# Second group's context and normalized x: turned by 128-byte loads and VectorE's 32x32 transposes in place of TensorE

## Chip, core and metric

The kernel runs on one core of a Trainium2 chip. The metric is the device time of one execution in microseconds (us), as the median of several runs. Everything is float32. The engines of the core are TensorE (PE in the profile; PEld is its weight load), VectorE (DVE), ScalarE (ACT), GpSimd (POOL) and SyncE (SP, which issues all DMA transfers of this kernel on one queue).

## What is computed

A cross-attention block: 8 sequences of 256 tokens (`x`), with a context of 256 tokens each, width 512, 16 heads of 32, and a hidden layer of 2048. Cut to what matters:

```python
B, LQ, _ = hidden_states.shape
residual = hidden_states
x = layer_norm(hidden_states, ln1_w, ln1_b)
q = (x @ q_w + q_b).reshape(B, LQ, H, HD).transpose(0, 2, 1, 3)
k = (encoder_hidden_states @ k_w + k_b).reshape(B, LK, H, HD).transpose(0, 2, 1, 3)
v = (encoder_hidden_states @ v_w + v_b).reshape(B, LK, H, HD).transpose(0, 2, 1, 3)
scores = jnp.einsum('bhqd,bhkd->bhqk', q, k) * scale
scores = jnp.where(mask, scores, mask_value)
attn = jax.nn.softmax(scores, axis=-1)
out = jnp.einsum('bhqk,bhkd->bhqd', attn, v)
out = out.transpose(0, 2, 1, 3).reshape(B, LQ, D)
hidden = out @ cproj_w + cproj_b + residual
y = layer_norm(hidden, ln2_w, ln2_b)
y = jax.nn.gelu(y @ fc_w + fc_b, approximate=True)
return hidden + y @ proj_w + proj_b
```

## The kernel before

The eight sequences are worked in two groups of four (g = 0 and 1), 1024 tokens each. For each group: the context and the normalized x are brought into a layout with the features on the partitions ("turned"), then come the projections k, v and q, sixteen attention units, the output projection `o`, the second layer norm, and the two layers `fc` and `pd`. The matrix products are done with Strassen's scheme of seven products (`quad`): a product is called `k1_0_P1` (group 1, part 0, product 1) and so on, and the sums it needs are called `c1t1`, `x1t2`, `kws1`, `fw0s1`, `z0t1` (outer sums) and `fw0i1_1`, `y0i1_1`, `z0i1_1` (inner sums). Product results are evicted from PSUM by DVE or ACT (`_t1`, `_c11`, `_c22` and so on), and some later additions may go to DVE or POOL.

An attention unit has a number of three digits (group, head group, sequence): `s101` are its scores on PE, `ev` the evictions with the mask on ACT, `mx`, `mt`, `mc` and `fold` the maximum over the keys on DVE and ACT, `md` a store of that maximum to memory and `mm` a load that spreads it over all partitions, `less` the subtraction on POOL or DVE, `exp` the exponential on ACT, `av` the value product and the row sums on PE, `r` and `att` the division on DVE. Three further units are scored before a unit's `av`.

How the turn was done for group 1: the context came as eight tiles of 128 tokens (`ct1_0` to `ct1_7`, rows of 2 KB). `turned` (L711) runs for each of four 128-wide blocks of features (a) and each half of the tokens (L) four 128x128 transposes on PE against the identity into one PSUM bank (L728, operation `turn_c1_aL`), and an eviction of 128x512 to SBUF (L608, `c1_aL`, ACT or DVE). For x, tiles `xt1_0` to `xt1_7` are normalized in token layout (`norm_x1`, L807 on ACT or L809 on DVE) and then turned in the same way (`turn_x1_aL`), with the layer norm's weight and bias applied in the eviction (`x1_aL`, L764 on ACT, L766 on DVE).

A second way to turn is already there, `moved` (L732), used for y of group 1: the normalized tiles are stored to memory (`yd1_0` to `yd1_7`), read back in pieces of 32 features (128 bytes) so that each 32x32 block lies on the right partitions (`yb1_ca`, sixteen loads of 128 KB), turned block by block on DVE (`yT1_cL`, L747), and scaled in place (`y1_cL`, L751 on ACT, L753 on DVE). All loads are issued at L595, all stores at L601.

What sets the order: the string `PROGRAM` lists all operations in one sequence, with a letter for the engine where there is a choice (V for DVE, A for ACT, G for POOL). Each engine, and SP, takes its operations in this order; an operation that waits holds back all behind it on its engine. `PLACES` gives each buffer its slot in SBUF or its PSUM bank. Both tables are written out in the file.

Of the kernel before, what the change touches and what calls it, by code (L numbers as in the profile page):

```python
# [124 lines left out]
cq0_00_0 cq0_00_1 kw00 vw00 cq0_01_0 rows8 cq0_01_1 mk turn_c0_00 cq0_10_1 turn_c0_10 c0_00:V cq0_10_0 c0_10:A  # L125
cq0_11_0 small k0_0_P1 vw01 rows4 v0_0_P1 vw11 rows6 cq0_11_1 turn_c0_11 xt0_0 turn_c0_01 c0_11:V v0_1_P1 rows1
rows3 turn_c0_30 rows2 k0_1_P1 c0_30:V vw10 c0_01:V rows7 rows0 v0_0_t1:V turn_c0_20 rows5 turn_c0_21 c0_20:V kw01
turn_c0_31 c0t1:V fw0_11_1 v0_0_P2 c0_31:A kw10 c0_21:A vws1:V v0_1_t1:A kw11 fw0_10_0 stats_x0_00 c0t2:G v0_1_P2
v0_0_c11 xt0_7 mk~1 fw0_00_0 k0_0_P2 fw0_00_1 v0_1_c11 fw0_11_0 vws2:V kws3:V fw0_10_1 v0_1_P6 vws4:V xt0_3 kws1:V
fw0_01_1 xt0_1 cols v0_0_P6 v0_1_t2:A cols~1 fw0_01_0 c0t3:V xt0_2 fw1_00_0 c0t4:V k0_1_P2 v0_0_t2:A vd0_0_11  # L130
k0_1_t1:A xt0_5 fw0i1_1:V k0_0_t1:A kws2:V fw1_11_0 k0_0_P7 stats_x0_31 fw1_00_1 fw0s3:V k0_1_P6 fw0s1:V fw0i2_1:V
k0_1_P7 fw0i5_3:G k0_1_t2:A fw0s2:V k0_1_P5 fw0i7_1:V fcd0_6_False stats_x0_01 fw0i6_3:G xt0_6 fw0i5_1:V
fcd0_7_False k0_1_c11 fw0i6_1:G k0_0_P6 fw1_11_1 k0_0_c11 fw0i5_2:G fw1_01_0 stats_x0_21 fw0i6_2:G kd0_0_11
aggr_x0_01 aggr_x0_00 v0_1_P5 fw0i1_2:V k0_0_t2:A fw0s4:G k0_1_t3:A k0_1_c22 k0_0_P5 stats_x0_30 aggr_x0_30
stats_x0_10 fw0i6_4:G stats_x0_11 k0_1_P4 fw0i7_2:G k0_0_t3:A fcd0_6_True xt0_4 kws4:V fw1_01_1 aggr_x0_10
aggr_x0_11 v0_1_t3:V v0_0_P5 xt1_2 fw0i1_4:V aggr_x0_31 fcd0_5_False eps_x0_1 k0_0_c22 pow_x0_1 aggr_x0_21 k0_0_P4
fw0i2_3:V fw0i2_2:V eps_x0_3 nb_x0_1 eps_x0_0 stats_x0_20 fw0i2_4:G norm_x0_10:A fw0i7_3:V v0_0_t3:A v0_1_P3
fcd0_2_True pow_x0_0 k0_0_c21 norm_x0_11:A fw1_10_1 pow_x0_3 qw11 nb_x0_0 aggr_x0_20 nb_x0_3 eps_x0_2 k0_1_P3 qw10
fw0i7_4:V norm_x0_30:A pow_x0_2 qw00 norm_x0_00:A fw1i1_1:V qw01 fw1i4_3:G norm_x0_01:A fw1_10_0 k0_0_P3 nb_x0_2
fw0i5_4:G k0_1_c12:A norm_x0_20:A fw1i1_3:G fcd0_5_True turn_x0_00 fcd0_7_True fw0i1_3:G norm_x0_21:A k0_0_c12:V  # L140
turn_x0_30 kd0_1_11 qws1:G x0_00:A v0_0_P3 fcd0_1_True norm_x0_31:A kd0_1_12 vws3:V ct1_7 k0_1_c21 fw1i4_1:G
turn_x0_20 kd0_0_21 turn_x0_10 x0_30:V kd0_1_21 turn_x0_01 x0_10:A x0_20:V ct1_1 turn_x0_31 x0_01:A turn_x0_21
qws2:V turn_x0_11 v0_1_c12:V q0_0_P1 x0_11:A fw1i2_1:V fw1i4_2:V x0_31:A fw1i4_4:V v0_0_c12:V x0_21:A q0_1_P1
x0t1:V x0t2:V q0_1_P2 q0_1_t1:A x0t3:V q0_0_P2 fw1s1:V fw1i2_2:V q0_0_t1:A fcd1_5_False q0_1_P6 fw1i5_3:G xt1_3
fw1i2_3:V fcd1_4_True qws3:G q0_1_c11 ku031 q0_0_c11 q0_0_P6 x0t4:V s000 q0_0_t2:A fw1s3:V q0_0_P7 fw1s2:V ev000_31
fcd1_7_False q0_1_t2:A ev000_11 fw1i5_1:V fcd1_6_False fw1i6_1:G q0_0_P5 fcd0_3_False fw1i5_2:V fw1s4:G q0_1_P5
# [202 lines left out]
tr1_23 pd13_P4 out1_31:V pd17_11~1:G so1_33 pd12_P4 pd17_12~1:G so1_31 pd13_c21 tr1_13 so1_00 tr1_22 so1_03 pd14_t1  # L349
so1_01 pd14_P6 pd12_c21 tr1_10 tr1_12 out1_10:V pd14_P2 out1_11:V out1_21:V so1_10 pd14_t2 so1_13 pd14_P5 so1_32  # L350
so1_02 so1_21 pd14_P7 so1_12 pd14_t3 pd14_c11 so1_23 so1_30 so1_20 pd14_P3 pd14_c22 so1_11 so1_22 pd14_P4 pd14_c12
turn_o00 pd14_c21 ot00 turn_o10 turn_o11 ot10 turn_o01 ot11 st0 ot01 st1
"""

PLACES = """
# [1114 lines left out]
```

## Time and profile before

| | |
|---|---|
| median of three runs | 677.62 us (677.07 to 677.84) |
| profiled execution, its own time | 679.25 us |
| its span, first to last instruction | 677.5 us |
| granted TensorE clock | 0.999 |
| PE, DVE, ACT, POOL busy | 666.5, 589.9, 334.8, 347.6 us |
| DMA packets, bytes | 173033, 140.64 MB |
| packets under 512 bytes | 83713 |

In the profile a row of a group of instructions names line, engine, operation, what is written from what, the shapes and the count; then the busy time and the mean of one in ns; then the idle time of the engine just ahead of them and what ended it. Names of tiles are those of buffers, and a slot of SBUF goes by the name of its first user, so that `kw` or `xt` can stand for a later tile in the same place. In the row of a window, each engine has its busy time and in brackets its instructions; behind them stand the granted clock, the mean busy share of the sixteen DMA engines and the GB/s that they moved.

### The profile page before, as it was taken

The numbers are of one execution on the slowest core, as the hardware profiler recorded it, in microseconds if no ns is written. First come the engines' busy times: TensorE is split into PE (matmuls) and PEld (weight loads), VectorE is DVE, ScalarE is ACT, GpSimd is POOL, SyncE is SP. The second block draws the span as 40 slices with busy tenths as digits, with TensorE's granted clock in tenths as the row PEclk, the third lists the DMA queues.
The fourth block names the chain that finished last, engine by engine and source line by source line (L and its number), as shares of the span: only waits on it lengthen the run. The fifth ranks groups of instructions, "written<-read, shape, count | busy, mean of one in ns | idle before, by whom it ended". The sixth has DMA issues, their size and how long they took to land.

```text
span 677.5 us, 11498 instructions
## 1 busy us (share of the span) xinstructions
PE 666.5 (98%) x4001; PEld 498.2 (74%) x4001; DVE 589.9 (87%) x981; ACT 334.8 (49%) x691; POOL 347.6 (51%) x329
## 2 busy tenths in 40 slices
PE   9999999999999999999999999999999999999997
PEld 7656474478544776767687788888888888888885
DVE  1979989789999999999999999988677869999794
ACT  1244588678899979965874582011021003930000
POOL 0282563632879997689686924221398332300150
PEclk9999999999999999999999999999999999999999
DMA  7898885522445457796878769698998778434966
GB/s 239 290 303 315 292 319 191 184 87 79 134 165 164 141 159 236 244 288 218 257 226 270 225 164 284 173 290 306 138 240 262 183 175 224 118 90 124 228 164 117
DMA packets 173033, 140.64 MB, mean 208 GB/s; under 512 B 83713, under 2 KB 133425, under 8 KB 172977
## 3 DMA queue, kind: packets, MB, share of 16 engines
q1 hardware_dynamic: 172976, 139.92, 70.6%
q8 instruction: 32, 0.52, 0.3%
q14 instruction: 25, 0.20, 0.1%
HBM read 102.00 MB, written 37.88 MB: 206 GB/s over the span
## 4 chain that ended last, share of the span: by engine, by line
PE 73%; DVE 13%; ACT 5%; issue 3%; DMA 3%; POOL 2%; SPq 0%; DVEq 0%; POOLq 0%; ACTq 0%
PE pd_X L641 14%; PE fc_X L641 12%; PE pd_W L641 7%; PE fc_W L641 6%; DVE mx L1004 4%; PE av L641 4%; PE k_X L641 4%; PE pd_Y L641 4%; PE fc_Y L641 4%; PE v_X L641 3%; ACT pr L621 2%; PE s L641 2%; PE o_X L641 2%; PE k_W L641 2%; DVE h L632 2%
## 5 line engine op out<-in xcount | busy, mean ns | idle before, releaser
L621 ACT ACTIVATE pr<-s,cols 128x256 f32<-128x256 f32 x256 | 103.9, 482 | 28.2 <-PE s L641 19.6
L1029 POOL TENSOR_TENSOR pr<-pr,mm 128x512 f32<-128x512 f32 x80 | 100.5, 1284 | 8.3 <-DMA mm<-md 8.2
L1209 ACT ACTIVATE h<-h,cols 128x256 f32<-128x256 f32 x128 | 53.8, 497 | 51.1 <-DVE h L632 51.0
L1004 DVE TRANSPOSE_TENSOR_REDUCE mx<-pr 128x32 f32<-128x1024 f32 x64 | 77.5, 1223 | 1.6 <-DMA md<-mx 0.8
L1032 ACT ACTIVATE pr<-pr 128x1024 f32<-128x1024 f32 x64 | 66.5, 1061 | 8.7 <-POOL pr L1029 5.3
L632 DVE TENSOR_TENSOR h<-fc_X,h 128x512 f32<-128x512 f32 x80 | 53.0, 681 | 10.2 <-PE fc_X L641 8.9
L641 PE MATMUL av<-pr,ones 128*32 128x256 f32 x512 | 34.2, 384 | 2.3 <-ACT pr L1032 1.9
L632 DVE TENSOR_TENSOR h<-fc_W,h 128x512 f32<-128x512 f32 x48 | 32.0, 678 | 2.9 <-PE fc_W L641 2.9
L630 POOL TENSOR_TENSOR z1i<-z1t,z1t 128x512 f32<-128x512 f32 x2 | 2.5, 1268 | 55.8 <-DVE z1t L632 55.8
L1024 DVE TENSOR_TENSOR pr<-pr,mm 128x1024 f32<-128x1024 f32 x24 | 29.6, 1253 | 0.5 <-DMA mm<-md 0.5
L641 PEld LDWEIGHTS av<-pr,ones 128*32 128x32 f32 x512 | 14.1, 109 | 20.4 <-issue 6.0
L807 ACT ACTIVATE xn_y<-hid,rs_y 128x512 f32<-128x512 f32 x12 | 9.4, 812 | 37.6 <-DVE rs_y L799 32.4
L1011 ACT COPY mx<-mx 32x64 f32<-32x64 f32 x96 | 23.3, 243 | 7.9 <-DVE mx L1008 5.6
L641 PE MATMUL pd_W<-z1i,pl 128*128 128x256 f32 x104 | 24.4, 379 | 0.0
L641 PE MATMUL pd_X<-z0i,pl 128*128 128x256 f32 x96 | 22.5, 380 | 0.0
L641 PE MATMUL pd_X<-z1i,pl 128*128 128x256 f32 x96 | 22.2, 381 | 0.0
L641 PEld LDWEIGHTS pd_W<-z1i,pl 128*128 128x128 f32 x104 | 19.8, 190 | 2.7
L1012 DVE TENSOR_REDUCE mx<-mx 32x32 f32<-32x256 f32 x32 | 18.4, 574 | 3.8 <-ACT mx L1011 3.8
L641 PE MATMUL pd_W<-z0i,pl 128*128 128x256 f32 x88 | 20.7, 380 | 0.2 <-issue 0.2
L641 PEld LDWEIGHTS pd_X<-z1i,pl 128*128 128x128 f32 x96 | 18.0, 190 | 3.1 <-issue 0.4
L641 PEld LDWEIGHTS pd_X<-z0i,pl 128*128 128x128 f32 x96 | 18.2, 190 | 2.9 <-DVE po L853 0.4
L632 POOL TENSOR_TENSOR po<-po,e 128x256 f32<-128x256 f32 x12 | 10.3, 874 | 18.4 <-DVE e L632 11.6
(585 smaller groups left out, 1815.6 us busy)
## 6 DMA issues: line engine op xcount, KB each, us to landing
mm<-md SPq DMA_DIRECT2D x32, 512.0 KB, 4.5
pl<-prd SPq DMA_DIRECT2D x63, 256.0 KB, 3.4
fl<-fcd SPq DMA_DIRECT2D x33, 256.0 KB, 4.8
fw<-in_L_xattn_fc_w_dram SPq DMA_DIRECT2D x16, 256.0 KB, 5.0
pw<-in_L_xattn_proj_w_dram SPq DMA_DIRECT2D x32, 128.0 KB, 3.6
hid<-in_x_dram SPq DMA_DIRECT2D x8, 512.0 KB
hd<-hid SPq DMA_DIRECT2D x8, 512.0 KB, 5.5
fcd<-fw0i SPq DMA_DIRECT2D x7, 512.0 KB, 7.2
```

The lines of the kernel that those rows point to most:

```text
L621: lambda e: nc.scalar.activation(to(), of_(), AF.Identity, bias=bias(), scale=1.0))
L630: nc.gpsimd.tensor_tensor(to()[:, ts(k, 512)], in0()[:, ts(k, 512)], in1()[:, ts(k, 512)], op)
L632: E[e].tensor_tensor(to(), in0(), in1(), op)
L641: nc.tensor.matmul(o(), l(), r(), start=first, stop=True, skip_group_check=True)
L807: nc.scalar.activation(tile_of(xn), f(), AF.Identity, bias=tile_of(rs)[:, 4 + i : 5 + i], scale=tile_of(rs)[:, 2 + i : 3 + i])
L1004: T.op(f"mx{u}_{h}", [("DVE", 1.126)], [(pr[h], None)], [(mx, [h])], lambda e, h=h: nc.vector.tensor_reduce(tile_of(mx)[:, 0:64].rearrange ...
L1011: lambda e, a=a: nc.scalar.copy(tile_of(mx)[0:32, 64 + 64 * a : 128 + 64 * a], tile_of(mx)[32 * a : 32 * a + 32, 64:128]))
L1012: T.op(f"fold{u}", [("DVE", 0.38)], [(mx, [2, 3, 4, 5])], [(mx, [6])], lambda e: nc.vector.tensor_reduce(tile_of(mx)[0:32, 320:352], tile_ ...
L1024: nc.vector.tensor_tensor(p_, p_, m_[:, :, None, :].to_broadcast([P, 2, 2, S]), ALU.subtract)
L1029: E[e].tensor_tensor(p_, p_, at(M, j)[:, None, :].to_broadcast([P, 2, S]), ALU.subtract)
L1032: lambda e, h=h: nc.scalar.activation(tile_of(pr[h]), tile_of(pr[h]), AF.Exp), table="exp")
L1209: lambda e, f=f, b=b, c=c: nc.scalar.activation(at(h[f][b], c), at(h[f][b], c), AF.Gelu_apprx_tanh, bias=col(c_fcb + f * 4 + c), scale=1.0 ...
```

## The change

`attention_inputs` no longer calls `turned` for group 1.

- The context of group 1 is read by a new function, `fetched`: sixteen loads of 128 KB straight from the input, in pieces of 128 bytes (`cb1_ca`; c is the block of 128 features, a the 32 features within it), and eight DVE transposes of 128x512 in 32x32 blocks (`cT1_cL`), which write the turned tensor. The eight tile loads, eight groups of PE transposes and eight evictions are gone.
- The normalized x of group 1 goes through `moved`: eight stores (`xd1_0` to `xd1_7`, 256 KB each), sixteen loads of 128-byte pieces (`xb1_ca`), each of which needs all eight stores, eight DVE transposes (`xT1_cL`), and eight scalings in place (`x1_cL`, six on ACT and two on DVE).
- `PROGRAM` and `PLACES` are other tables: 2951 operations in place of 2927, in another order from the third on, 222 of the kept ones on another engine (from POOL to DVE 88, DVE to POOL 84, DVE to ACT 31, ACT to DVE 19).

```diff
+    def fetched(g, tag, src):
+        R = [[Buf(f"{tag}{g}_{J}{L}", "Q", 4) for L in range(2)] for J in range(2)]
+        for c in range(4):
+            q = Buf(f"{tag}b{g}_{c}", "Q", 4)
+            for a in range(4):
+                load(f"{tag}b{g}_{c}{a}", q, [a], lambda q=q, a=a: tile_of(q)[32 * a : 32 * a + 32].rearrange("p (t j) -> p t j", j=32),
+                     lambda a=a, c=c: src[ts(g, 1024), :].rearrange("(t i) (b a j) -> b a i t j", i=32, b=4, a=4)[c, a], 0.33, lead=2.0)
+            for L in range(2):
+                r, j = R[c // 2][L], c % 2
+                T.op(f"{tag}T{g}_{c}{L}", [("DVE", 0.6)], [(q, None)], [(r, [2 * j, 2 * j + 1])],
+                     lambda e, q=q, r=r, j=j, L=L: nc.vector.transpose(at(r, j, 1, 512), at(q, L, 1, 512)))
+        return R
...
-        ct = token_quarters(g, "c", ef) if g == 0 else token_tiles(g, "c", ef)
         if g == 0:
+            ct = token_quarters(g, "c", ef)
             biases()
-        C = turned(g, "c", ct if g == 0 else [(b, lambda b=b: tile_of(b)) for b in ct], plain)
+        C = turned(g, "c", ct, plain) if g == 0 else fetched(g, "c", ef)
...
-        X = turned(g, "x", xn, scaled(c_ln1w, c_ln1b))
+        X = moved(g, "x", xn, c_ln1w, c_ln1b) if g else turned(g, "x", xn, scaled(c_ln1w, c_ln1b))
...
 PROGRAM = """
-cq0_00_0 cq0_00_1 kw00 vw00 cq0_01_0 rows8 cq0_01_1 mk turn_c0_00 cq0_10_1 turn_c0_10 c0_00:V cq0_10_0 c0_10:A
+cq0_00_0 cq0_00_1 mk cq0_10_1 cq0_10_0 rows8 rows2 vw00 turn_c0_10 cq0_01_0 turn_c0_00 c0_10:A cq0_01_1 c0_00:V rows6
```

Three places show the order. The first is PE, between the scores of unit 022 and those of unit 010, before. `ps_c_11` and `ps_c_01` are the PSUM banks of the turned context, `v_1_W` a product of v of group 0.

```order
L641 MATMUL s_3_889<-q_0_22_733,k_0_22_491 128x256
L728 MATMUL ps_c_11_900<-ident,xt_5_409 128x128
L728 MATMUL ps_c_11_900<-ident,xn_x_10_527 128x128
L728 MATMUL ps_c_11_900<-ident,ct_6_814 128x128
L728 MATMUL ps_c_11_900<-ident,k_0_22_491 128x128
L641 MATMUL v_1_W<-vw_259,c0t_399 128x256 x4
L728 MATMUL ps_c_01_922<-ident,xt_5_409 128x128
```

The same place now:

```order
L640 MATMUL s_3_888<-q_0_22_738,kw_320 128x256
L640 MATMUL v_1_W<-vws_323,c0t_339 128x256 x4
L640 MATMUL v_0_W<-vw_294,c0t_360 128x256 x4
L640 MATMUL v_1_W<-vw_294,c0t_360 128x256 x4
L640 MATMUL s_0_949<-q_0_11_680,xt_2_370 128x256
```

All eight groups of transposes of the context stood here; now three products stand between the two scores.

The second is SP, around the maximum of unit 001 (`md_154`, stored, and the `mm` read back from it), before. `pw` is a weight of the second layer, `ku` keys that are read back.

```order
L595 DMA ku_1508<-kd_1_22_129 128x256
L595 DMA ku_1510<-kd_1_11_126 128x256
L595 DMA ku_1523<-kd_0_22_125 128x256
L601 DMA md_154<-mx_1446 32x32
L595 DMA mm_1603<-md_154 128x1024
L595 DMA pw_00_1605<-in_L_xattn_proj_w_dram 128x2x128
```

And now, with the stores of x (`xd_162`) and the loads of its pieces (`xb_c`):

```order
L600 DMA xd_162<-xt_7_1098 128x512
L600 DMA xd_162<-kw_282 128x512
L594 DMA ku_1473<-kd_1_11_126 128x256
L594 DMA vu_1477<-vd_0_12_131 128x2x128
L600 DMA md_154<-mx_1429 32x32
L594 DMA xb_2_1505<-xd_162 32x32x32
L594 DMA xb_0_1513<-xd_162 32x32x32
L594 DMA ku_1515<-kd_1_21_128 128x256
L594 DMA xb_2_1505<-xd_162 32x32x32
L594 DMA mm_1521<-md_154 128x1024
```

The read-back of the maximum now stands behind three loads of pieces, the first of which needs the last store of x.

The third is DVE, where the last of x was evicted before (`x_11` and `x_01` from their PSUM banks):

```order
L632 TENSOR_TENSOR v_1_11_1503<-v_1_Y,v_1_11_1503 128x512
L1024 TENSOR_TENSOR pr_0_1413<-pr_0_1413,mm_1603 128x1024
L766 TENSOR_SCALAR x_11_1655<-ps_x_31_1640,cols 128x512
L766 TENSOR_SCALAR x_01_1663<-ps_x_01_1650,cols 128x512
L1024 TENSOR_TENSOR pr_1_1399<-pr_1_1399,mm_1603 128x1024
```

and where it is turned now, ahead of the first product of q of group 1:

```order
L759 STREAM_TRANSPOSE x_01_1693<-xb_1_1676 128x512
L759 STREAM_TRANSPOSE x_00_1781<-xb_1_1676 128x512
L765 TENSOR_SCALAR x_00_1781<-x_00_1781,cols 128x512
L631 TENSOR_TENSOR xt_1_1149<-v_0_W,xt_1_1149 128x512
L759 STREAM_TRANSPOSE x_11_1740<-xb_3_1743 128x512
L1024 TENSOR_REDUCE mx_1714<-mx_1714 32x32
L759 STREAM_TRANSPOSE x_10_1664<-xb_3_1743 128x512
```

Two evictions stood here; now four transposes and a scaling do, each transpose behind the loads of its block.

More of the change, by code (lines that the diff above doesn't have):

```diff
@@ L130 @@
[L130 to L134, printed above, removed]
@@ L350 @@
[L350 to L352 removed]
+cq0_00_0 cq0_00_1 mk cq0_10_1 cq0_10_0 rows8 rows2 vw00 turn_c0_10 cq0_01_0 turn_c0_00 c0_10:A cq0_01_1 c0_00:V
+rows6 cq0_11_1 cq0_11_0 turn_c0_20 vw01 turn_c0_30 c0_20:V small v0_1_P1 kw10 mk~1 c0_30:V rows5 vw10 v0_0_P1 kw00
```

668 lines of the change are left out of this document (337 added, 331 removed).

## The prediction

> **What bounds the kernel now.** I read the page first: the span, the busy shares, the slices.
>
> ```profile
> span 677.5 us, 11498 instructions
> PE 666.5 (98%) x4001; PEld 498.2 (74%) x4001; DVE 589.9 (87%) x981; ACT 334.8 (49%) x691; POOL 347.6 (51%) x329
> DVE  1979989789999999999999999988677869999794
> DMA  7898885522445457796878769698998778434966
> ```
>
> TensorE (PE) is busy 98% of the span, VectorE (DVE) 87%, and in the middle of the run DVE stands at nine tenths too. The busy shares of five stretches (length, then PE, PEld, DVE, ACT, POOL, granted clock, DMA share, GB/s) show which is where.
>
> ```profile
> 0.00:160.00 160.00, 158.42 (x919) 97.67 (x920) 129.85 (x232) 92.25 (x187) 68.07 (x76) 1.00 0.71 239
> 256.00:340.00 84.00, 82.06 (x744) 57.68 (x743) 81.62 (x152) 65.65 (x130) 67.18 (x71) 1.00 0.79 249
> 440.00:660.00 220.00, 219.97 (x1011) 190.60 (x1010) 184.25 (x300) 43.57 (x92) 76.44 (x74) 1.00 0.77 195
> 85.00:105.00 20.00, 19.57 (x152) 13.48 (x151) 17.91 (x28) 17.21 (x44) 14.95 (x15) 1.00 0.85 309
> 140.00:160.00 20.00, 19.86 (x143) 15.60 (x142) 17.93 (x39) 15.34 (x34) 2.07 (x3) 1.00 0.24 80
> ```
>
> Up to 160 us PE is full and DVE has 30 us free; from 256 to 340 us DVE has 2.4 us free and PE 1.9; from 440 us PE is full and DVE has 36 us free. So PE sets the pace at both ends, and DVE holds it in the late scores of group 1. The waits of PE are small; the longest two end on the softmax and on a POOL addition (total, times, longest):
>
> ```profile
> PE av L641 <- ACT pr L1032: 1.9, 2, 1.4
> PE fc_W L641 <- POOL h L632: 0.8, 1, 0.8
> ```
>
> **What PE loses.** The timeline of PE (start, duration) around the last transposes of x, and the chain of waits (last row) later:
>
> ```profile
> 160.47 0.27 PE L728 MATMUL ps_x<-ident,xt 128*128 128x128 f32 x1
> 162.10 0.27 PE L728 MATMUL ps_x<-ident,kws 128*128 128x128 f32 x1
> 162.21 3.62 PE L641 MATMUL v_X<-vws,c 128*128 128x256 f32 x16
> 165.76 1.15 PE L641 MATMUL s<-q,ku 32*128 32x256 f32 x16
> 166.84 1.99 PE L641 MATMUL v_W<-vw,c1t 128*128 128x256 f32 x8
> 168.67 1.89 PE L641 MATMUL v_W<-xt,c1t 128*128 128x256 f32 x8
> 451.50 10.36 PE pd_X L641 x48
> ```
>
> Sixteen transposes run from 160.47 to 162.21, 0.109 us each. The change removes 64 (two tensors, eight groups of four): 7.0 us. Against this, the new order goes more often between full products and the row-wise scores or column-wise value products: I count 107 such changes in it, 97 before. A step of eight takes 1.73 us inside a run (10.36 for 48) and 1.83 us behind a score (166.84 to 168.67), so a change costs 0.1 us and ten more cost 1.0. PE has 6.0 us less to do.
>
> **What DVE and ACT get.** The groups of instructions (busy, mean ns of one):
>
> ```profile
> L747 DVE STREAM_TRANSPOSE y<-yb 128x512 f32<-128x512 f32 x8 | 5.4, 688 | 0.0
> L608 DVE COPY c<-ps_c 128x512 f32<-128x512 f32 x8 | 5.4, 680 | 13.6 <-PE ps_c L728 13.6
> L766 DVE TENSOR_SCALAR x<-ps_x,cols 128x512 f32<-128x512 f32 x5 | 3.9, 797 | 0.4 <-PE ps_x L728 0.4
> L608 ACT COPY c<-ps_c 128x512 f32<-128x512 f32 x8 | 4.6, 588 | 15.8 <-PE ps_c L728 15.8
> L751 ACT ACTIVATE y<-y,cols 128x512 f32<-128x512 f32 x7 | 5.5, 811 | 20.5 <-DVE y L747 20.5
> L753 DVE TENSOR_SCALAR y<-y,cols x1: 499/499/499, 494.8 to 494.8; 128x512 f32<-128x512 f32 x1
> ```
>
> The same turn exists already for y of group 1, so its price is in the trace. DVE gains 16 transposes at 0.69 (11.0) and two scalings at 0.50 (1.0), and loses three evictions of c at 0.68 and three of x at 0.80 (4.4): 7.6 us more. ACT loses five copies at 0.59 and keeps the scalings, six instead of five at 0.81: it has half its time free. The rest of the order pays DVE's 7.6 back: `less` 24 to 22 on DVE, `xb` 5 to 2, the outer sums `z` 30 to 25, more of others. Adding all DVE instructions of each order with the durations of their groups gives 635.8 us before and 634.7 now (durations overlap, so the sum stands above the 589.9 busy). In total DVE is even; what matters is where.
>
> ```profile
> 256.73 1.15 PE L641 MATMUL s<-vws,k 32*128 32x256 f32 x16
> 336.32 1.15 PE L641 MATMUL s<-q,k 32*128 32x256 f32 x16
> ```
>
> These are the scores of unit 101 and of unit 133, the last, 79.6 us apart: the stretch that DVE holds. In it DVE has 83.4 us of durations before and 87.2 now (four more statistics of y and three aggregates, two more first evictions of fc), so 0.954 us of time for each, and 83.2 us now: 3.6 longer, where PE has 2.8 more. Ahead of unit 101 PE has 16 groups of transposes fewer (-7.0), one step of 1.73 fewer and eight changes of mode more (+0.8): -7.9. DVE has 4.2 us fewer durations there, so it does not take that back. Behind unit 133 PE has one step of 0.87 fewer: -0.9. Sum: -7.9 + 3.6 - 0.9 = -5.2.
>
> **What the DMA queue and SP get.** Issue to landing, and three windows of 5 us around y's turn:
>
> ```profile
> yb<-yd SPq DMA_DIRECT2D x16, 128.0 KB, 4.4
> yd<-xn_y SPq DMA_DIRECT2D x7, 256.0 KB, 5.4
> 470.00:475.00 5.00, 5.00 (x25) 4.41 (x24) 2.39 (x3) 0.47 (x1) 2.19 (x2) 1.00 0.93 301
> 480.00:485.00 5.00, 5.00 (x25) 4.41 (x24) 3.30 (x7) 0.00 (x0) 0.47 (x1) 1.00 1.42 146
> ```
>
> With whole rows a full queue moves 301 GB/s, with the 128-byte pieces 146. A tensor of 2.1 MB so takes 14.4 us instead of 7.0. Context of group 1 costs the queue 7.4 us more; x a store of 7.0 and a load of 14.4, 21.4 more. The x pieces fall where the queue is busy 24% (140 to 160 us, above), so they lie beside other work; without that room they would cost the 21.4. The context pieces fall ahead of 105 us, into a queue at 85%: 15% of some 100 us is free, twice what they need. Ahead of `xb1_22` SP now waits for the last `xd1` to land, 5.4 us after its issue; two PE steps (3.5 us) lie between, so SP stands about 2 us, and behind it the pieces, `ku031` and the maximum of unit 001 (`mm001`). Fourteen PE steps and scores, some 21 us, lie between `mm001` and its `av001`: hidden, or 2 us if not.
>
> The tight place is the first softmax:
>
> ```profile
> 82.43 7.01 DMA md<-mx
> 89.52 0.32 SPq L595 DMA_DIRECT2D mm<-md  x1
> 93.55 4.97 POOL L1029 TENSOR_TENSOR pr<-pr,mm 128x512 f32<-128x512 f32 x4 [1.34 <-DMA mm<-md]
> 102.65 1.86 PE av L641 x32
> L1032 ACT ACTIVATE pr<-pr 128x1024 f32<-128x1024 f32 x64 | 66.5, 1061 | 8.7 <-POOL pr L1029 5.3 <-DVE pr L1024 3.3
> ```
>
> Store and load of the maximum of unit 000 pass a queue full of stores: 7.0 us, then 4.0. POOL subtracts 5.0, ACT's exponential takes 1.1: ready at 99.6, wanted at 102.65, 3.0 us spare. Eight of the removed groups of transposes stood in that gap: the work that is taken away was itself the cover. Before, PE had three scores, eight turns and four steps between `mm000` and `av000` (3.3 + 3.5 + 6.9 = 13.7 us); now it has two scores and five steps (2.2 + 8.6 = 10.8). 2.9 of the 3.0 are gone. If the queue is as late as before, PE loses nothing; if it is 1 to 3 us later, PE stands that long; if it is earlier (fewer stores lie ahead of this maximum than before), still nothing is won. I take 0.6, ends 0 and 3.
>
> The forecast: -5.2 + 0.6 = -4.6 us. The profiled run took 679.25 us for its span of 677.5; the sum is made against the span, 672.9, which is 674.6 as a profiled run and 677.62 - 4.6 = **673.0** against the median.
>
> **Rivals.**
> *PE alone counts.* DVE follows in the late scores, since it got 30 us of room early and can work ahead. Then -6.0 and no new stall: 677.6 - 6.0 = 671.6; 670 if the 1.9 us of old waits at value products go too. For it: equal DVE totals. Against: 2.4 us free in 84.
> *DVE takes it back.* If DVE needs not 0.954 but full durations in the stretch (+3.8) and again behind it, where up to the first steps of `pd02` DVE's durations run 7.3 us ahead of PE's, 0.7 before, then another 6.6 x 0.93 = 6.1 us come on top: 678, no change. For it: additions with both inputs in SBUF are dearer here when POOL works:
>
> ```profile
> L632 DVE TENSOR_TENSOR h<-h,e 128x512 f32<-128x512 f32 x5 | 4.7, 930 | 0.0
> ```
>
> 0.93 against 0.68 for evictions; five outer sums go from POOL to DVE. [...] Against: DVE has 36 us free behind 440.
> *The queue falls behind (slower).* Place: `md` and `mm` of units 000 to 022, behind 128-byte pieces and stores of `fcd`. It decides once `mm000` lands more than 0.1 us later than before; then everything behind `av000` inherits it, since PE takes its work in order. If all 7.4 us of extra queue time ahead of 105 us arrive at `av000`, PE loses 7.3 there; and x's last loads have two value products, a step and a score (6.3 us) between them and the first product of q, for 4.4 of landing and two transposes on DVE: another 1 to 2 if they are as late. 677.6 - 6.0 + 7.3 + 1.5 = 680.4, with an open end upward. For it: 7.0 us landing of 4 KB at 82 us; queue above 0.85. Against: 15% free.
> [...]
>
> *The change doesn't do what it says.* Excluded: the 64 transposes are gone from PE's list.
>
> **How the numbers follow.** Forecast 0.45 (671.5 to 675.5), PE alone 0.12 (669.5 to 671.5), DVE takes it 0.17 (675.5 to 679), queue 0.26 (679 to 688). A measurement here tells 0.2%, 1.4 us, from no change: faster is below 676.3. That is forecast, PE alone and a sixth of DVE's: 0.60; same is most of DVE's and a little of the queue's, 0.13; slower 0.27. The range 669.5 to 684 leaves out a twentieth below and a tenth above; the likeliest's own is 671.5 to 675.5.
>
> **What would show it.** PE busy near 660 and 3937 matmuls; scores of unit 101 near 249 us and of unit 133 near 332; DVE over 97% busy between them; a wait of PE at the first `av` under 1 us; 128-byte loads landing in 4 to 5 us, x's in a queue under 80%. Wrong would be: PE idle over 4 us ahead of 110 us (queue), or unit 133 later than 335 us (DVE), or unit 101 later than 252.

## The result, and the profile after

The changed kernel takes 670.76 us (median of nine runs, 668.47 to 675.55) where the kernel before takes 677.23 (nine runs, 676.17 to 678.58): a ratio of 0.9913, 95% interval 0.9888 to 0.9938, so 4.2 to 7.6 us faster: 6.5 us between the medians, 5.9 by the ratio, which is one of means. The forecast was 673.0. The profiled execution took 672.14 us for a span of 670.3, against 679.25 and 677.5 before.

The page of the changed kernel, the same lines as before:

```profile
span 670.3 us, 11469 instructions
PE 658.5 (98%) x3937; PEld 491.4 (73%) x3937; DVE 590.8 (88%) x986; ACT 340.0 (51%) x700; POOL 358.8 (54%) x323
DVE  2989799989999999999999999998688868897985
DMA  8998988578647447787788876978977986538756
```

PE does 64 matmuls fewer and is busy 8.0 us less, DVE is busy 0.9 us more: the turn has moved from an engine that is full to one that was "even" in total. The span is 7.2 us shorter. Where, is read from three windows, cut at the scores of unit 101 and of unit 133 (length, then busy time of PE, PEld, DVE, ACT and POOL, clock, DMA share, GB/s). Before:

```profile
0.00:256.73 256.73, 253.47 (x1673) 157.54 (x1673) 222.92 (x376) 177.64 (x374) 148.83 (x135) 1.00 0.62 205
256.73:336.32 79.59, 77.65 (x714) 54.26 (x713) 77.21 (x147) 62.03 (x122) 62.89 (x67) 1.00 0.78 245
336.32:677.50 341.18, 335.34 (x1617) 286.37 (x1616) 289.79 (x460) 95.12 (x198) 135.85 (x128) 1.00 0.76 201
```

The changed kernel:

```profile
0.00:248.78 248.78, 245.25 (x1602) 147.92 (x1602) 221.31 (x371) 178.43 (x376) 148.33 (x132) 1.00 0.76 225
248.78:333.31 84.53, 80.93 (x725) 57.15 (x724) 80.31 (x153) 64.20 (x124) 69.03 (x73) 1.00 0.77 242
333.31:670.30 336.99, 332.36 (x1613) 286.32 (x1612) 289.14 (x464) 97.39 (x202) 141.43 (x121) 1.00 0.77 203
```

Up to unit 101 it gains 7.95 us, in the late scores it gives 4.94 back, and behind unit 133 it gains 4.19 again. In the first stretch PE's records fall by 71 and its busy time by 8.2: the gain there is PE's work. In the middle both PE (+3.3) and DVE (+3.1) have more to do. PE's 11 records more there are those that the two other stretches lose beside the 64 transposes (7 and 4): work that the new order has moved, not new work. Behind unit 133 PE has four records fewer, 0.9 us, but 4.2 us less time: that is the part that needs explaining.

The first value product, where the forecast feared the queue. The timeline of the changed kernel (start, duration; the store of the maximum of unit 000, its load, the subtraction, the second exponential, the product):

```profile
78.67 0.70 SPq L600 DMA_DIRECT2D md<-mx  x1
82.23 0.34 SPq L594 DMA_DIRECT2D mm<-md  x1
86.12 5.02 POOL L1041 TENSOR_TENSOR pr<-pr,mm 128x512 f32<-128x512 f32 x4 [0.94 <-DMA mm<-md]
92.31 1.06 ACT L1044 ACTIVATE pr<-pr 128x1024 f32<-128x1024 f32 x1
94.36 1.07 PE L640 MATMUL av<-pr,ones 128*32 128x256 f32 x16
```

The same exponential before:

```profile
100.88 1.10 ACT L1032 ACTIVATE pr<-pr 128x1024 f32<-128x1024 f32 x1
```

Before, it ended at 101.98 and the product began at 102.65: 0.7 us to spare, not the 3.0 that the prediction worked out from POOL's end. Now it ends at 93.37 and the product begins at 94.36 without a wait: 1.0 us to spare. The load is issued 3.6 us after the store instead of 7.1. So the cover did shrink (from the store to the product 15.7 us instead of 20.2), but the maximum's way through the queue shrank with it.

The 128-byte loads (KB each, median us from issue to landing), the transposes and DVE's two scalings of x (busy, mean ns, idle before), in the changed kernel:

```profile
cb<-in_ctx_dram SPq DMA_DIRECT2D x16, 128.0 KB, 4.0
xb<-xd SPq DMA_DIRECT2D x16, 128.0 KB, 3.6
```

```profile
L742 DVE STREAM_TRANSPOSE c<-cb 128x512 f32<-128x512 f32 x8 | 5.2, 674 | 0.0
L759 DVE STREAM_TRANSPOSE x<-xb 128x512 f32<-128x512 f32 x8 | 5.4, 686 | 0.0
L765 DVE TENSOR_SCALAR x<-x,cols 128x512 f32<-128x512 f32 x2 | 2.1, 1026 | 0.0
```

The transposes cost what was forecast (0.69 us), the loads land a little sooner than the 4.4 us of y's; a scaling on DVE took 1.03 us, twice its price.

### The profile page after: what moved, and what is told of

The parts are those of the page before. It is cut to its first block, busy times and chain, and to the rows that moved or that the text cites. A ratio compares the mean times of both kernels' runs of the same rounds, so it can differ in the third digit from the quotient of the medians.

```text
span 670.3 us, 11469 instructions
## 1 busy us (share of the span) xinstructions
PE 658.5 (98%) x3937; PEld 491.4 (73%) x3937; DVE 590.8 (88%) x986; ACT 340.0 (51%) x700; POOL 358.8 (54%) x323
## 4 chain that ended last, share of the span: by engine, by line
PE 73%; DVE 15%; DMA 3%; ACT 3%; issue 2%; SPq 1%; POOL 0%; DVEq 0%; ACTq 0%
PE pd_X L640 14%; PE fc_X L640 13%; PE pd_W L640 7%; PE fc_W L640 7%; DVE mx L1016 4%; PE v_X L640 4%; PE pd_Y L640 4%; PE av L640 3%; PE fc_Y L640 3%; PE k_X L640 2%; PE s L640 2%; PE q_X L640 2%; PE o_X L640 2%; PE k_W L640 2%; PE o_W L640 2%
## 5 line engine op out<-in xcount | busy, mean ns | idle before, releaser
L1041 POOL TENSOR_TENSOR pr<-pr,mm 128x512 f32<-128x512 f32 x84 | 110.0, 1342 | 27.7 <-DMA mm<-md 20.4
L631 POOL TENSOR_TENSOR tq<-tq,rq 128x512 f32<-128x512 f32 x9 | 11.8, 1313 | 32.9 <-PE pd_X L640 13.0
L640 PE MATMUL fc_X<-y1i,fl 128*128 128x256 f32 x96 | 24.4, 382 | 0.1
L607 ACT COPY e<-fc_X 128x512 f32<-128x512 f32 x5 | 2.9, 581 | 40.9 <-DMA fl<-fcd 31.6
L763 ACT ACTIVATE y<-y,cols 128x512 f32<-128x512 f32 x6 | 4.9, 812 | 35.9 <-DMA yb<-yd 20.0
L629 POOL TENSOR_TENSOR z0t<-h,z0t 128x512 f32<-128x512 f32 x6 | 7.6, 1282 | 27.6 <-DVE z0t L631 19.1
L640 PE MATMUL fc_W<-y1i,fl 128*128 128x256 f32 x84 | 20.8, 380 | 0.0
L640 PEld LDWEIGHTS fc_X<-y1i,fl 128*128 128x128 f32 x96 | 17.9, 190 | 3.4 <-DVE fl L607 0.5
L1396 POOL TENSOR_TENSOR hid<-hid,cb 128x1024 f32<-128x1024 f32 x6 | 15.4, 2578 | 6.6 <-DMA hid<-in_x_dram 6.6
L640 PE MATMUL pd_X<-z0i,pl 128*128 128x256 f32 x80 | 18.6, 379 | 0.0
```

What stands on the lines that cost most here:

```text
L629: nc.gpsimd.tensor_tensor(to()[:, ts(k, 512)], in0()[:, ts(k, 512)], in1()[:, ts(k, 512)], op)
L631: E[e].tensor_tensor(to(), in0(), in1(), op)
L640: nc.tensor.matmul(o(), l(), r(), start=first, stop=True, skip_group_check=True)
L1041: E[e].tensor_tensor(p_, p_, at(M, j)[:, None, :].to_broadcast([P, 2, S]), ALU.subtract)
L1396: lambda e, v=v: E[e].tensor_tensor(v(), v(), cb.t[:, None, :].to_broadcast([P, 2, D]), ALU.add), lock=True)
```

## The experiments

Twelve kernels, all but one built from the changed kernel; each was timed against the kernel before on the same chip. The chips differ from group to group, so a distance from the changed kernel is taken from the ratios (their difference, in us of 677.2), which fixes it to about 2 us: the last column.

| run | edit, in short | median us | ratio to before, 95% interval | later than the change, us |
|---|---|---|---|---|
| (the change) | | 670.76 | 0.9913 (0.9888 to 0.9938) | 0 |
| e1 | PE work added | 682.19 | 1.0069 (1.0055 to 1.0084) | +10.6 |
| e2 | new DVE transposes twice | 685.54 | 1.0126 (1.0106 to 1.0145) | +14.4 |
| e3 | whole rows for 128-byte pieces | 672.03 | 0.9921 (0.9903 to 0.9938) | +0.5 |
| e4 | pieces twice | 682.64 | 1.0080 (1.0058 to 1.0101) | +11.3 |
| e5 | late DVE work added | 684.18 | 1.0100 (1.0087 to 1.0114) | +12.7 |
| e6 | late DVE work taken away | 672.41 | 0.9918 (0.9898 to 0.9938) | +0.3 |
| e7 | two stores ahead of the first maximum | 671.17 | 0.9901 (0.9886 to 0.9917) | -0.8 |
| e8 | context half undone | 676.17 | 0.9984 (0.9974 to 0.9994) | +4.8 |
| e9 | 16 additions divided as before | 675.15 | 0.9961 (0.9944 to 0.9977) | +3.3 |
| e10 | the kernel before, additions divided as after | 676.45 | 0.9983 (0.9971 to 0.9995) | |
| e11 | one late store moved | 675.75 | 0.9965 (0.9952 to 0.9978) | +3.5 |
| e12 | all 16 additions on GpSimd | 673.01 | 0.9925 (0.9902 to 0.9949) | +0.8 |

### e1: is TensorE's time what counts?

```diff
-                for j in range(2)
+                for j in ((0, 0, 0, 0, 0, 1) if p == 1 and name[:2] in ("k1", "q1") else (0, 1))
```

> The changed kernel with 16 more matmuls of TensorE: the first 128x512 product of the first step of each k and q of group 1 is done five times instead of once (same result), 16 x 0.43 = 6.9 us, near the places where the transposes stood. If TensorE sets the pace up to unit 101 and its lost time counts in full: the score of unit 101 at 248.8 + 6.9 = 255.7, and the end later by 5 to 7 us, near 676 to 678. If VectorE holds the run from 105 us on, it uses the time to get ahead and most comes back in the late scores: the end later by 0 to 3 us, 671 to 674.

```profile
0.00:262.22 262.22, 259.12 (x1633) 154.18 (x1634) 220.46 (x371) 178.47 (x376) 150.56 (x131) 1.00 0.72 213
262.22:345.62 83.40, 80.59 (x726) 56.46 (x725) 79.54 (x153) 64.13 (x124) 69.16 (x73) 1.00 0.77 246
```

The same windows, up to unit 133. The price in the expectation was half of the true one: one 128x512 product is two records of 0.43 us, so 16 of them are 32 records (3969 in all against 3937) and 13.9 us of busy time in the first stretch. The score of unit 101 is 13.4 us later and the end 12.2 in the profiled pair, 10.6 by the ratios: between three quarters and nine tenths of the added work arrive at the end. The late scores take 83.4 us, 0.1 less than in any other run that leaves them as they are (83.5 to 84.8), although DVE had 13 us longer for what lies ahead of them. TensorE's time counts for the most part; VectorE does not use the time to get ahead by more than that.

### e2, e3, e4: do DVE's transposes and the small pieces lie beside other work?

e2, in `fetched`, and in `moved` for x:

```diff
-                     lambda e, q=q, r=r, j=j, L=L: nc.vector.transpose(at(r, j, 1, 512), at(q, L, 1, 512)))
+                     lambda e, q=q, r=r, j=j, L=L: [nc.vector.transpose(at(r, j, 1, 512), at(q, L, 1, 512)) for _ in range(1 if tag == "y" else 2)])
```

> The changed kernel with each of the 16 new VectorE transposes done twice: 16 x 0.69 = 11.0 us of VectorE more, half of it at 89 to 103 us (21 us free in the first 105), half at 158 to 177 us, where VectorE is 91 to 98% busy. If TensorE sets the pace: the context half is hidden, of the x half one or two us show, the end at 671 to 673. If VectorE holds the pace from 105 us on: 5.5 x 0.95 = 5.2 us more at least, 676; with both halves 10.5 us, 681.

Above both of the outcomes that were named: 14.4 us later than the changed kernel for 11.0 us of added work. The timeline of PE at the first place (in brackets the wait and what ended it), and three windows of 3.41 us there, a length that the last section comes back to:

```profile
99.74 5.40 PE L640 MATMUL k_X<-c,kw 128*128 128x512 f32 x8 [2.21 <-DVE v L631]
105.07 1.15 PE L640 MATMUL s<-xt,kws 32*128 32x256 f32 x16
```

```profile
96.55:99.96 3.41, 1.20 (x21) 0.54 (x14) 3.34 (x6) 2.06 (x7) 3.41 (x4) 1.00 0.02 1
99.96:103.37 3.41, 3.41 (x5) 1.35 (x5) 3.34 (x9) 2.97 (x6) 2.79 (x3) 0.50 0.55 201
103.37:106.78 3.41, 3.41 (x22) 1.58 (x22) 3.34 (x5) 0.49 (x2) 0.00 (x0) 1.00 0.98 272
```

The first products of k of group 1 stand 2.2 us, and then run at half the clock: eight records take 5.40 us where they take 3.70 in the changed kernel. The next score is 5.2 us later, for the five extra transposes that DVE had done by then (3.4 us): 3.3 us are waits (1.04 at 91.6 us and the 2.21) and 1.7 the lower clock. At 177.6 us PE stands again, 3.17 us, behind the transposes of x. DVE's 21 free microseconds up to 105 us (84.0 busy in the changed kernel) lay mostly earlier in the run, not behind these transposes: what stands next in its list is late at once. So the change's own transposes caused no wait, but had no slack either.

e3, both kinds of loads (the x half alike, from `d.t`):

```diff
-                load(f"{tag}b{g}_{c}{a}", q, [a], lambda q=q, a=a: tile_of(q)[32 * a : 32 * a + 32].rearrange("p (t j) -> p t j", j=32),
-                     lambda a=a, c=c: src[ts(g, 1024), :].rearrange("(t i) (b a j) -> b a i t j", i=32, b=4, a=4)[c, a], 0.33, lead=2.0)
+                load(f"{tag}b{g}_{c}{a}", q, [a], lambda q=q, a=a: tile_of(q)[32 * a : 32 * a + 32],
+                     lambda a=a, c=c: src[ts(g, 1024), :].rearrange("(c a i r) d -> c a i (r d)", c=4, a=4, i=32)[c, a], 0.33, lead=2.0)
```

> The changed kernel with the 32 loads of context and x of group 1 taken in pieces of 4 KB instead of 128 bytes: same bytes, tiles and order; keys, values and queries of group 1 are then made from elements in other places. If the small pieces lie wholly beside other work: no change, within 1.5 us of the changed kernel's 670.8. If they cost time (the queue is 92% busy in the first 105 us): 3 us less or more, down to 14.8 less if all their extra time of 2 x 7.4 us counted. The loads should land about 1 us sooner.

```profile
cb<-in_ctx_dram SPq DMA_DIRECT2D x16, 128.0 KB, 3.3
xb<-xd SPq DMA_DIRECT2D x16, 128.0 KB, 2.6
```

The loads land 0.7 and 1.0 us sooner and the time does not move (the intervals of 0.9921 and 0.9913 cover each other). The small pieces cost the change nothing that can be measured; a cost below some 1.5 us would not show.

e4, behind each of these loads:

```diff
+            if twice:
+                nc.sync.dma_start(again[name].t.rearrange("p (t j) -> p t j", j=32), of_())
```

> The changed kernel with a second copy behind each of the 32 loads, of the same 128-byte pieces into a scratch tensor in HBM that nothing reads: the queue's work for the pieces is at least doubled, 2 x 14.4 us more. If the queue had room for the change: up to 105 us 8 us are free (92% busy), so 6 us or more overflow there and the first value product (94.4 us in the changed kernel) waits 2 to 6 us; from 105 to 160 us 14 us are free and it is hidden. So 673 to 677. If the queue has far more room than its busy share says: within 1 us. If SyncE or the queue are full already: later by 10 us or more.

Later by 11.3 us, the third of the outcomes. PE waits 3.5 us up to 97 us, and 0.6, 1.9 and 2.6 us between 178 and 193 us; the last row is DVE's:

```profile
97.05 3.78 PE L650 MATMUL v_W<-vw,c0t 128*128 128x256 f32 x8 [3.52 <-DVE k L641]
100.77 2.09 PE L650 MATMUL s<-q,xt 32*128 32x256 f32 x16
...
182.89 1.26 PE L650 MATMUL s<-q,ku 32*128 32x256 f32 x16 [1.86 <-DMA ku<-kd]
...
192.24 1.94 PE L650 MATMUL av<-pr,ones 128*32 128x256 f32 x16 [2.60 <-DVE att L641]
...
188.79 0.71 DVE L769 STREAM_TRANSPOSE x<-xb 128x512 f32<-128x512 f32 x1 [4.13 <-DMA xb<-xd]
```

```profile
97.00:102.80 5.80, 5.75 (x27) 3.75 (x27) 4.87 (x7) 3.58 (x7) 5.80 (x5) 0.50 0.79 175
...
184.00:186.00 2.00, 2.00 (x36) 1.00 (x33) 0.66 (x2) 2.00 (x3) 2.00 (x2) 1.00 1.06 166
```

So the queue took the pieces once, and not twice. The late pieces reach PE through DVE's list: a transpose that has to wait for its piece (4.13 us at 188.8; another stands 2.65 us at 95.7, where the profile names a store of weight sums) holds back the evictions and divisions behind it, and PE waits for those. The copies also double what SyncE has to issue for the pieces, so which of the two ran out, SyncE's list or the queue, e4 does not separate; that the room was the 15% that the prediction found is not shown. The waits of 3.5 and 2.6 us are followed by half the clock, the wait of 1.9 us is not.

### e5, e6: does VectorE hold the late scores?

e5 does each statistic of y of group 0 three times, e6 takes it over 64 of 512 columns:

```diff
-                     lambda e, i=i, f=f, st=st: nc.vector.bn_stats(tile_of(st)[:, 6 * i : 6 * i + 6], f()))
+                     lambda e, i=i, f=f, st=st: [nc.vector.bn_stats(tile_of(st)[:, 6 * i : 6 * i + 6], f()) for _ in range(3 if f"{tag}{g}" == "y0" else 1)])
```

```diff
-                     lambda e, i=i, f=f, st=st: nc.vector.bn_stats(tile_of(st)[:, 6 * i : 6 * i + 6], f()))
+                     lambda e, i=i, f=f, st=st: nc.vector.bn_stats(tile_of(st)[:, 6 * i : 6 * i + 6], f()[:, :64] if f"{tag}{g}" == "y0" else f()))
```

> The changed kernel with each of the eight statistics of y of group 0 done three times: 16 x 0.68 = 10.9 us of VectorE more between 240 and 265 us, five eighths of it (6.8) behind the score of unit 101. If VectorE holds the late scores, as forecast (0.95 us of time for each us of its work): the score of unit 133 later by 6.5 us or more, the end by 6 to 10 us, 677 to 681. If the stretch is set by TensorE's own work and by waits for single scores, and VectorE only looks full because it follows: the end later by 0 to 4 us, 671 to 675.

> The changed kernel with the eight statistics of y of group 0 taken over 64 of the 512 columns (so the normalization of y of group 0 uses part of each row): 4 to 5 us of VectorE less between 240 and 265 us. If VectorE holds the late scores: the score of unit 133 sooner by 3 us, the end by 3 to 4, 667 to 668. If it only follows: within 1 us of the changed kernel, 670 to 672.

The late scores of e5, and two waits of PE there:

```profile
254.67:346.76 92.09, 83.65 (x726) 57.44 (x725) 88.42 (x165) 63.25 (x122) 66.16 (x70) 0.97 0.69 218
```

```profile
252.13 2.61 PE L640 MATMUL o_W<-vws,a0t 128*128 128x256 f32 x8 [2.05 <-DVE hid L631]
...
270.60 2.44 PE L640 MATMUL av<-pr,ones 128*32 128x256 f32 x14 [4.84 <-ACT pr L1044]
```

The late scores of e6:

```profile
251.06:334.37 83.31, 80.56 (x726) 56.69 (x725) 77.25 (x153) 63.76 (x124) 69.25 (x73) 1.00 0.78 245
```

Added: DVE is busy 8.1 us more in the stretch (88.42 against 80.31) and the stretch is 7.6 us longer, 0.93 us for each, part of it the lower clock after the long waits; the end is 12.7 us later, above both of the outcomes that were named. Taken away: DVE is busy 3.1 us less (77.25) and the stretch is 1.2 us shorter than the changed kernel's, which is no more than it varies by from run to run (83.4 to 84.8); the end does not improve. That is the outcome named for a VectorE that only follows. So more work of VectorE lands on the path, but less does not shorten it: with 3 us less the stretch is 83.3 us, of which PE is busy 80.6.

### e7: the cover of the first softmax

```diff
-ev020_30 md000 fcd1_3_False fw1i6_3:V mx020_1 fw1i7_2:G fcd1_7_False q0_1_P7
+ev020_30 fcd1_3_False fw1i6_3:V mx020_1 fw1i7_2:G fcd1_7_False md000 q0_1_P7
```

> The changed kernel with one thing moved in SyncE's list: two stores of weight sums (512 KB each), which stood behind the store of the maximum of unit 000, stand ahead of it. The maximum then lands 3 to 4 us later, the second exponential of unit 000 is ready 3 to 4 us later, and the first value product, which had 1.0 us to spare (exponential ready at 93.4, product at 94.4), waits 2 to 3 us; the clock then stays low for some us, as in the two runs with long waits, another 1 to 2 us. If this cover is as thin as that and the delay is inherited to the end: later by 3 to 5 us, 674 to 676. If the chain has room, or what is late at 94 us is made up for later: within 1 us.

```profile
79.47 0.82 SPq L600 DMA_DIRECT2D md<-mx  x1
83.54 0.34 SPq L594 DMA_DIRECT2D mm<-md  x1
...
93.00 1.06 ACT L1044 ACTIVATE pr<-pr 128x1024 f32<-128x1024 f32 x1 [0.30 <-POOL pr L1041]
94.11 1.07 PE L640 MATMUL av<-pr,ones 128*32 128x256 f32 x16
```

The store of 4 KB passed the megabyte ahead of it with only 0.5 us more (4.1 us from issue to load instead of 3.6); the exponential ended at 94.06 and the product began at 94.11. The spare went from 1.0 to 0.05 us and no wait came. The edit was too weak to show what a wait here would cost; that stays open. Two stores of 512 KB ahead of it cost this maximum 0.5 us; why it took 7.1 us in the kernel before stays open too.

### e8: the context half undone

```diff
-cT1_00
+turn_c1_00 c1_00:A
...
-cT1_11
+turn_c1_10 c1_10:V
...
-k1_0_P1
+k1_0_P1 turn_c1_01 c1_01:V turn_c1_11 c1_11:A turn_c1_21 c1_21:A turn_c1_31 c1_31:V c1t1:G
...
-        C = turned(g, "c", ct, plain) if g == 0 else fetched(g, "c", ef)
+        C = turned(g, "c", ct if g == 0 else [(b, lambda b=b: tile_of(b)) for b in token_tiles(g, "c", ef)], plain)
```

> The changed kernel with the context half undone, the x half left: context of group 1 comes in whole rows (eight loads), is turned by 32 transposes of TensorE (3.5 us) and leaves PSUM by eight evictions (five by ScalarE, three by VectorE); four of the eight turns stand ahead of the first value product, as in the kernel before, four behind the first product of k. If TensorE's lost work is what the change gains: the score of unit 101 later by 3.5 us, the end near 674.3. If the small pieces and the transposes of VectorE cost as much as TensorE gains: within 1 us of the changed kernel. If the gain comes from the new order alone: the same, within 1 us.

```profile
0.00:254.03 254.03, 250.01 (x1633) 151.48 (x1633) 217.34 (x366) 181.36 (x381) 148.36 (x131) 1.00 0.70 220
```

In the profiles 4.1 us are lost (674.4 against 670.3), by the ratios 4.8: PE is busy 4.8 us more in the first stretch, 3.5 of them the transposes, and stands 1.1 us at 90 us for a bank of theirs. DVE is busy 4.0 us less there and it helps nothing. So undoing the context half takes back most of the change's gain, and it is TensorE's work that does it. Of the 5.9 us, 1.1 (0.4 to 1.8) are left with the x half and the new order, although x takes as many transposes off PE. The x half was not undone alone, and no run has the new order with all the transposes or the old order without them, so what the order costs or gains by itself is not shown.

### e9, e10, e12: the gain behind unit 133

In the changed kernel 4 of the 16 additions h + e of the seventh products are on VectorE and 12 on GpSimd; before it was 8 and 8. e9 gives the changed kernel the division of before (ten letters change), e10 the reverse, e12 puts all on GpSimd. One of e9's letters:

```diff
-fc007_11~1:G
+fc007_11~1:V
```

> The changed kernel with the sixteen additions h + e of group 0's seventh products divided between VectorE and GpSimd as in the kernel before: 8 on VectorE and 8 on GpSimd, instead of 4 and 12; their places in the order stay. These lie between 365 and 400 us. If the 3.3 us that the changed kernel gains behind unit 133 beyond its one product less come from this division (VectorE's evictions of fc come in time, TensorE's steps start without a gap): the end later by 1 to 3 us, 672 to 674, with gaps before products of fc near 370 to 385 us. If they come from elsewhere in the order: within 1 us of 670.8.

> The kernel before with the same sixteen additions divided as in the changed kernel: 4 on VectorE, 12 on GpSimd. If the division is what costs the kernel before its 1.0 us at 376 us (a wait of 0.82 and a late step) and some of its late steps behind it: the end sooner by 1 to 2 us, 675.5 to 676.5. If not: within 0.7 us of the kernel before, 677.4; if GpSimd's longer list holds products back instead, later.

> The changed kernel with all sixteen additions h + e of group 0's seventh products on GpSimd (the changed kernel has four of them on VectorE); places in the order stay. If what helps behind unit 133 is VectorE freed of additions with two inputs in SBUF, four more off it bring up to 1 us: 669.8 to 670.8. If GpSimd's list becomes the late one (4 x 1.3 us more in 100 us of which it is busy 54): waits of TensorE or ScalarE on GpSimd's h, later by 0 to 2 us, 671 to 673.

e9, the last stretch, the larger group of the additions on DVE in it (busy, mean ns, idle before), and two weight loads of TensorE there:

```profile
333.72:673.30 339.58, 333.74 (x1613) 285.69 (x1612) 294.45 (x468) 97.49 (x202) 138.05 (x117) 1.00 0.75 201
```

```profile
L631 DVE TENSOR_TENSOR h<-h,fl 128x512 f32<-128x512 f32 x6 | 4.9, 822 | 0.0
...
372.40 0.73 PEld L640 LDWEIGHTS fc_X<-y0i,fl 128*128 128x128 f32 x4 [0.47 <-DVE h L631]
373.49 0.73 PEld L640 LDWEIGHTS fc_X<-y0i,qw 128*128 128x128 f32 x4 [0.36 <-DVE h L631]
```

e10, the last stretch:

```profile
333.43:674.30 340.87, 335.87 (x1617) 286.05 (x1616) 289.19 (x456) 95.28 (x198) 142.41 (x132) 1.00 0.75 201
```

e9 is 3.0 us longer than the changed kernel in the profiles (673.3 against 670.3) and 3.3 by the ratios. It is 2.6 us longer behind unit 133, with the same 1613 records of PE: 1.4 us in busy time (a product that starts late shows as 1.13 us instead of 1.03) and 1.2 in waits. All of it arises between 372 and 401 us, where these additions lie. Additions with two inputs in SBUF take 0.82 us there against 0.68 for an eviction; DVE works without a gap, its evictions come late, and the weight loads of the next products wait for them, as the two rows show.

So in the changed order the old division costs 2.6 us. That does not make it the cause of the 4.2 us that this stretch gains: in the kernel before the new division brings only 0.3 us there (340.87 against 341.18). Where the gain lies says the same. Adding up by how much each of PE's records starts later than the usual distance behind the one before (0.216 us for a product of 128x256), PE is late by 11.8 us in this stretch before and by 8.4 in the changed kernel. Of these 3.4 us only 1.5 fall in the first 80 us, with the additions; 1.9 fall later, where e9 is no later than the changed kernel. Four records of PE are the other 0.9. What shortens the later part no run shows.

e10's median is 1.2 us below the kernel before, the interval 0.3 to 2.0, but the profile puts it in the first stretch, where nothing was changed, so it cannot be laid to the edit. e12 is no better than the changed kernel.

### e11: an attempt to take out the longest wait

```diff
-prd0_2_True
 att102
...
 mm101
+prd0_2_True
 fc001_t3:A
```

> The changed kernel with one store of weight sums (512 KB, to prd) moved in SyncE's list behind the load of the maximum of unit 101. In the changed kernel it stands there from 274.6 to 276.2 us for its last sum, and behind it wait two loads for the products of fc and the maximum's load; TensorE then waits 1.57 us at 281.6 for a product of fc and 0.77 us at 290.8 for the exponential of unit 101. If SyncE's stand is what makes these late: both waits shrink, together by 1 to 2.3 us, and the end is 668.5 to 669.8. If the loads are held by their tiles instead, or the time is given back: within 0.5 us.

PE and ACT in e11:

```profile
284.17 2.55 PE L657 MATMUL s<-vws,kws 32*128 32x256 f32 x16 [3.57 <-ACT pr L637]
```

```profile
282.06 0.84 ACT L637 ACTIVATE pr<-s,cols 128x256 f32<-128x256 f32 x2 [4.78 <-DMA prd<-pw0i]
```

Not as expected: 3.5 us slower than the changed kernel. The wait of 1.57 us is gone and one of 3.57 us came in its place, with half the clock behind it; the late scores take 89.1 us instead of 84.5. The chain of waits of the changed kernel already had the cause:

```profile
274.64 4.37 DMA prd<-pw0i
...
279.08 0.21 ACT pr L620
...
281.58 1.10 PE fc_W L640 x4
```

The store's tile is the next user's: ACT's evictions of unit 121 write into the slot that the store empties. The store, not the loads behind it, was the late one, and issuing it later made the evictions later.

## Why the prediction came out right, point by point

The sign and the size were right, for the forecast's main reason, that PE's lost transposes count. Two of its terms were off in opposite directions, by 1.3 and 3.3 us, so that the sum came as near as it did is in part luck.

| stretch | forecast | profiled pair |
|---|---|---|
| up to unit 101 | -7.9, and +0.6 at the first softmax | -7.95 |
| unit 101 to 133 | +3.6 | +4.94 |
| behind unit 133 | -0.9 | -4.19 |
| sum | -4.6 | -7.2; medians -6.5 |

The near agreement in the first row is partly luck. That stretch varies between executions: in the kernel before it is 256.73 us, in e10, which is the same up to there, 253.80; in the changed kernel and the five runs that change little ahead of unit 101 (e3, e7, e9, e11, e12) it is 247.4 to 250.2, mean 249.1 (251.1 in e6, which takes a little of DVE's work away there). From the means the gain is about 6.2 us. The middle is 83.4 to 84.8 us in the changed kernel and the runs that leave it as it is (e1, e3, e7, e8, e9), mean 84.1, so 4.5 us are lost there; the last is 336.4 to 337.4 wherever it was left as it is. From the means the sum is 6.2 - 4.5 + 4.2 = 5.9 us gained, as by the ratio of the runs.

*PE loses 7.0 us of transposes, and its time counts.* Shown both ways: e1 adds 13.9 us and 10.6 to 12.2 arrive, e8 gives half of the transposes back (3.5 us) and 4 to 5 us arrive, some of it as waits for their banks. The 1.0 us for ten more changes of mode did not show as a loss: PE's busy time fell by 8.0, not 6.0 (by 6.8 between e10 and e7, which differ by the change and little else); the runs scatter too much to price it.

*DVE holds the late scores.* Half right. The step as put, 0.954 us of time for each us of DVE's work, holds for work added (e5: 0.93) and not for work taken away (e6: 3.1 us less, and the stretch within its scatter). In the changed kernel DVE is busy 95% of the stretch, below the "over 97%" that was to show it, and PE 96%: the two hold it together. The prediction had PE's 2.8 us more there and let them vanish under DVE's 3.6; PE's busy time grew by 3.3, two thirds of the 4.94 that the stretch lost. The term was 1.3 us too small (0.9 from the means): PE's waits there grew from 1.9 to 3.6 us (length less busy time), 1.57 us of it behind the store of e11.

*The cover of the first softmax.* The step "3.0 us spare" misread the trace: the second exponential ended 0.7 us before its product. No wait came, inside the range that was named (0.6, ends 0 and 3), because the maximum passed the queue 3.5 us faster; with the 7.1 us of before and 1.0 us to spare, the product would have waited some 2.5 us, as an estimate from these rows. The prediction had thought of an earlier queue, with fewer stores ahead, but gave it no size and no weight: that no time was lost here is in part luck. What made the queue faster is not shown.

*Behind unit 133.* The term that was mis-sized: one step of PE, -0.9, was all that was counted, and 4.2 came. The rest is PE's steps starting on time more often, 1.5 us of it where the additions of e9 lie and 1.9 far behind. The prediction saw the moved additions only as a total of durations, "even", which says nothing of where they hold an eviction back. The direction in which it feared this place ("DVE's durations run 7.3 us ahead of PE's") did not show.

*What DVE and ACT get.* The scalings of x on DVE took 1.03 us each, not the 0.50 of the one of y that was read for them, so DVE's extra work was 1.1 us more than the 7.6; the rest of the order paid that too (DVE's busy time rose by 0.9 us in all).

*The rivals.* "DVE takes it back" was wrong where it put the loss, but its price was real: e2 and e5 show 14.4 and 12.7 us for some 11 us of DVE work. That the additions of its row are dearer when POOL works can be read in the trace of the kernel before: of the five, the two beside which POOL worked for less than a fifth of the time took 0.68 and 0.69 us (at 359.0 and 362.6 us), the three beside which it worked for half of it or more 1.24, 1.16 and 0.89 (at 382.1, 565.6 and 579.2 us). "The queue falls behind" had the mechanism: e4, with the pieces twice, is 11.3 us slower than the change; with the pieces once nothing shows (e3, in whole rows, comes out 0.5 us later than the change, inside the interval).

What stays open: what a wait at the first value product would cost, why the first maximum passes the queue faster, the shares of the x half and of the new order by itself, and what shortens the part behind the additions.

## What to carry to other kernels

Work taken from the engine that runs its list without gaps came back for the most part (in e1 10.6 to 12.2 us of 13.9), and a second engine at nine tenths did not prevent it. But that engine and the queue, which took the work once without a wait, charged for more at once (1.2 to 1.3 us for each further microsecond of VectorE's), so a busy share below one is no slack: look at the place where the work lands, and at what is next in that engine's list. When a change brings a new order, compare the stretches it does not speak of too: here 4.2 us were gained behind unit 133, and giving sixteen additions there their old division cost 2.6, though in the old order the new division brought 0.3. What that division of work among engines was worth depended on the order that it stood in. Look for the cause of the longest wait at the head of its chain: the load or bank that it names may itself stand behind a tile that a store has not left yet, here that of the store at 274.64 us, 4.37 us long.

## What the hardware showed that was not expected

Some waits of TensorE cost more than their length, and not by their length alone: half the clock followed a wait of 1.79 us (e4, in the first 8 us), and none a wait of 1.86 (e4, to 182.89 us). In e2, e4, e5 and e11 the granted clock fell and rose only at moments that lie a whole number of 3.41 us apart: in e2 it falls at 99.96 and 181.88 us and is full again at 103.37 and 185.29; the kernel before and the changed kernel had it full for 669.0 and 665.6 us, 196 and 195 times that. In slices of 3.41 us cut at these moments, over the fourteen profiles, the busiest slice that was followed by half the clock has 1.63 us of work (e4, the wait of 1.79 us at its start), the least busy whole one that was not has 1.73 (e3, a wait of 1.81 us). The first two rows are of e4, the third is of e3:

```profile
3.96:7.38 3.42, 1.63 (x15) 1.33 (x14) 0.69 (x1) 0.59 (x1) 0.00 (x0) 1.00 0.85 247
7.38:10.79 3.41, 3.41 (x28) 3.08 (x27) 1.50 (x3) 0.00 (x0) 0.00 (x0) 0.50 1.05 342
...
281.31:284.72 3.41, 1.73 (x8) 1.44 (x8) 3.31 (x6) 1.15 (x4) 2.75 (x3) 1.00 0.96 312
```

A wait of 1.86 us (e4, 181.02 to 182.89) fell across two slices and left the clock at 1.00; waits of 2.05 us (e5), 2.21 (e2) and 2.60 (e4) lay wholly or for the most part in one and halved it. The clock was full again after one slice, or after two (e4 from 96.12 to 102.95, e11 from 283.36 to 290.18) where the end of the wait had left PE 2.6 us of work or less in the first; with 2.87 (e4 at 191.70) one was enough. A full slice at half the clock cost 1.7 us (5.40 instead of 3.70 in e2), and a set of 16 score matmuls took 2.09 us instead of 1.15. e2 and e5 have two such slices each behind their edits, about 3.4 us; they lost 3.4 and 1.7 us more than the work that was added. What sets the 3.41 us, and where between 1.63 and 1.73 us of work the two kinds of slices part, no run was made to show.
